# One set of 21 on-chip slots for keys, values, probability parts and tail loads in a quantised attention and mixture-of-experts layer

## The chip, the cores and the metric

The kernel runs on one core of a Trainium2 chip. The core has a matrix engine (PE, with its weight loads shown as PEld), a vector engine (DVE), a scalar engine (ACT), a general engine (POOL) and a sync engine (SP), each with its own instruction stream, and 16 DMA engines that all of them may start transfers on. The on-chip memory SBUF has 128 partitions; a tile's size is given here per partition. The metric is the time of one execution on the device in microseconds (us).

## What is computed

A layer over 2,048 tokens of width 256. `x` is normalised and projected to queries, keys and values of 16 heads of 128 with 4-bit weights (codes times scales of blocks of 32); softmax attention; an output projection; a normalisation and the residual. Then a router picks two of eight experts, each a gated feed-forward of inner width 176; their weighted sum is normalised and added.

```python
def attn(x, ...):
    q = _mxfp4_matmul(x, wq_codes, wq_scales) + bq      # k, v alike; 16 heads of 128
    scores = jnp.einsum('bqhd,bkhd->bhqk', q, k) / jnp.sqrt(jnp.float32(HEAD_DIM))
    attn = jax.nn.softmax(scores, axis=-1)
    out = jnp.einsum('bhqk,bkhd->bqhd', attn, v).reshape(B, S, NUM_HEADS * HEAD_DIM)
    return _mxfp4_matmul(out, wo_codes, wo_scales) + bo

def ffn(x, Wr, Wg, Wu, Wd):
    probs = jax.nn.softmax(jnp.einsum('bsh,he->bse', x, Wr), axis=-1)
    topk_w, topk_idx = jax.lax.top_k(probs, 2)
    combine = ...                                       # normalised, one-hot by expert
    h = jax.nn.silu(jnp.einsum('bsh,ehi->besi', x, Wg)) * jnp.einsum('bsh,ehi->besi', x, Wu)
    return jnp.einsum('bse,besh->bsh', combine, jnp.einsum('besi,eih->besh', h, Wd))

x = x + _layernorm(attn(_layernorm(x), ...))
x = x + _layernorm(ffn(_layernorm(x), ...))
```

## The kernel before

**Numbers in two parts.** Queries, keys, values and probabilities are each kept as a high and a low half-precision part whose sum carries more digits. So a score is three matmuls (high by high, high by low, low by high: L483, L484, L487), and so is a product with the values.

**The main loop** (L740) runs over 256 units and two more that drain it. Unit `g` is head `h = g // 16` and query tile `t = g % 16` of 128 rows. The order of instructions on every engine is the order in which the code issues them; nothing reorders them later. In each unit:

- PE computes the first half of the scores (1,024 keys) into a pair of accumulator banks `s`, of which there are three pairs; DVE takes its row maximum (L488).
- DVE forms the reciprocal of the sum of the unit before (`recip`, L506 to L509), and writes the second half of the low part `pl` of the unit before that (`low_half(1, ...)`, L528). Then SP issues the DMA transpose of that `pl` into `ptl` (L534).
- ACT writes the high part `ph` of the unit before (L513), and SP issues its transpose into `pth` (L516).
- PE computes the second half of the scores; DVE takes the maximum (L488) and combines the two (L492); ACT takes two exponentials into `p` (L499), which also frees the two score pairs.
- DVE writes the first half of the low part `pl` of the unit before (`low_half(0, ...)`, L528).
- PE works on parts of the product with the values (`pv_part`, L554): one for every half unit, eight to a block of four query tiles, 13 half units behind the scores. They read `pth`, `ptl` and `v`.
- `fill` puts projections between: in heads 0 to 14 the keys and values of a coming head, in all heads the next queries. PE computes them, ACT copies them to `t32` (L234, L265), POOL splits them into the two parts (L235, L236, L266, L267).

**Head 15** has no next keys and values to project. Instead `late` (L709) starts the loads of the tail: in units 0, 2, 4, 6, 8 a piece of the output weights (`wos` from ACT's queue in four DMAs, L632; `woc` from SP's, L637), in units 7, 9, 10, 11 the gate weights `Wg` (`gu_raw`, L673), in unit 9 the output bias `crow` (L724), and in units 9 and 11 to 14 finished head outputs read back from DRAM (`oi`, L693). ACT and POOL split the gate weights in units 10 to 13 (L664, L666). In the first draining unit SP issues three more `oi`.

**The tail** projects the outputs back (`op_mm`, L823), normalises, routes, and runs gate, up (L969) and down (L1009) matmuls for four blocks of 512 tokens. It loads `Wu` (`ust`), `Wd` (`draw`, L1112), `x` again (`x1`) and the other `oi`.

**Slots.** A tile comes from a pool under a tag; the tag has a fixed number of slots, each as large as the largest tile of the tag. When the program is built, each tile is given a slot of its tag that is then free. On the chip its first write waits, by a semaphore, until the slot's previous tile has been read for the last time; for a tile that a DMA reads, until that DMA has finished. Before the change these tags matter:

| tag | slots | KB of a slot | tiles |
|---|---|---|---|
| `kT` | 8 | 4 | keys of 512 positions, two parts (2 KB); in head 15 and the tail also `wos`, `woc`, `gu_raw`, `oi`, `x1_0` |
| `v` | 8 | 4 | values of 512 positions for two heads; later `wo`, `o_last`, `xT0`, `lgT0`, `x1_1`, `y`, one `oi` |
| `ph` | 3 | 4 | high part of the probabilities of a unit |
| `pl` | 2 | 4 | low part |
| `raw`, `at` | 2 and 2 | 4 | in the tail: `Wu` and `Wd` as loaded; the projected outputs |

`kT`, `v`, `ph` and `pl` are 21 slots of 4 KB together. The functions that the change touches and what calls them:

Of the kernel before, what the change touches and what calls it, by code (L numbers as in the profile page):

```python
# [20 lines left out]
S = 2048  # L21
# [9 lines left out]
ISQ = 1.0 / 128.0 ** 0.5  # L31
XS = 1024.0
PS = 16384.0
POOL_COLS = 512


@with_exitstack
def sandwich(
# [169 lines left out]
    def proj_psum(tag):  # L208
        if tag == "s":
            return s_pair()[:, 0]  # L210
        return psA.tile([128, 512], F32, name="pj", tag=tag)

    def proj_qk(which, h, b, tag="pj", wide=None):
        w = W[(h // 2, which)]
        bias = bqs[:, IX[which], h : h + 1]
        ps = proj_psum(tag)
        col = bass.ts(h % 2, 128)
        n = 0
        for kc in range(2):
            for hl in range(2):  # L220
                nc.tensor.matmul(
                    ps, w[:, kc, col], xnT[:, 4 * b : 4 * b + 4, hl * 2 + kc, :],
                    start=(n == 0), stop=(n == 3),
                )
                n += 1
        t = kqv.tile([128, 2, 512], HP, name=which + "T", bufs=8 if which == "k" else 2)
        if wide is None:
            nc.scalar.activation(t[:, 0, :], ps, AF.Identity, bias=bias)
            pending.append(lambda: nc.vector.scalar_tensor_tensor(
                t[:, 1, :], ps, bias, t[:, 0, :], ALU.add, ALU.subtract  # L230
            ))
        else:
            t32 = wide.tile([128, 512], F32, name="t32")
            nc.scalar.activation(t32, ps, AF.Identity, bias=bias)  # L234
            nc.gpsimd.tensor_copy(t[:, 0, :], t32)  # L235
            nc.gpsimd.tensor_tensor(t[:, 1, :], t32, t[:, 0, :], ALU.subtract)  # L236
        (Q if which == "q" else K)[(h, b)] = t

    def proj_v(p, t0, n, tag="pj", wide=None):
        w = W[(p, "v")]  # L240
        ps = proj_psum(tag)
        for j in range(n):
            i = 0
            for kc in range(2):
                for hl in range(2):
                    nc.tensor.matmul(
                        ps[:, bass.ts(j, 256)], xnT[:, t0 + j, hl * 2 + kc, :],
                        w[:, kc, :], start=(i == 0), stop=(i == 3),
                    )
                    i += 1  # L250
        if t0 % 4 == 0:
            V[(p, t0 // 4)] = kqv.tile([128, 2, 4, 256], HP, name="v", bufs=8)
        v = V[(p, t0 // 4)]
        sl = slice(t0 % 4, t0 % 4 + n)
        psv = ps[:, : n * 256].rearrange("p (t d) -> p t d", d=256)
        if wide is None:
            nc.scalar.copy(v[:, 0, sl, :], psv)
            pending.append(lambda: nc.vector.tensor_tensor(
                v[:, 1, sl, :], psv, v[:, 0, sl, :], ALU.subtract
            ))  # L260
        else:
            t32 = wide.tile([128, 512], F32, name="t32")[:, : n * 256].rearrange(
                "p (t d) -> p t d", d=256
            )
            nc.scalar.copy(t32, psv)  # L265
            nc.gpsimd.tensor_copy(v[:, 0, sl, :], t32)  # L266
            nc.gpsimd.tensor_tensor(v[:, 1, sl, :], t32, v[:, 0, sl, :], ALU.subtract)  # L267
# [241 lines left out]
        nc.vector.reciprocal(m[:, 6:7], m[:, 5:6])  # L509

    def high_part(h, t, m, p):
        ph = soft.tile([128, S], HP, name="ph", bufs=3)
        nc.scalar.activation(ph, p, AF.Copy, scale=m[:, 6:7])  # L513
        if t % 4 == 0:
            PT[(h, t // 4)] = pt.tile([128, 4, 16, 128], HP, name="pth")
        nc.sync.dma_start_transpose(  # L516
            out=PT[(h, t // 4)][:, t % 4], in_=ph
        )
        return ph
# [2 lines left out]

    def low_half(half, h, t, m, p, ph):
        if half == 0:
            LOW[(h, t)] = soft.tile([128, S], HP, name="pl")
        pl = LOW[(h, t)]
        cs = bass.ts(half, 1024)
        nc.vector.scalar_tensor_tensor(  # L528
# [17 lines left out]
    def pv_part(h, b, e):  # L546
# [10 lines left out]
            )  # L557
        if e == 7:
            if (h, b) == (NH - 1, 3):
                o = kqv.tile([128, 2, 2, 256], HP, name="o_last", tag="v", bufs=8)  # L560
                ps2 = halves(ps)
                nc.scalar.activation(o[:, :, 0, :], ps2, AF.Copy, scale=1.0 / PS)
                nc.vector.scalar_tensor_tensor(
# [76 lines left out]
    def dequant_wo(j):  # L640
        sc, cd = wo_raw.pop(j)
        if j % 4 == 0:
            wo.append(kqv.tile([128, 8, D], BF, name="wo", tag="v", bufs=8))
        hs = slice(2 * (j % 4), 2 * (j % 4) + 2)
        nc.gpsimd.tensor_tensor(wo[j // 4][:, hs], cd, sc, ALU.mult)

# [39 lines left out]

    OIN = {}

    def load_oi(b, half, j, tag="kT"):
        oi = kqv.tile(  # L690
            [128, 4, 2, 256], HP, name="oi", tag=tag, bufs={"kT": 8, "v": 8}[tag]
        )
        nc.sync.dma_start(  # L693
            out=oi.rearrange("p h l q -> p (h l q)"),
            in_=ot_d[b][:, half, 4 * j : 4 * j + 4].rearrange("p h l q -> p (h l q)"),
        )
        OIN[(b, half, j)] = oi
# [11 lines left out]
    def late(t):  # L709
        nonlocal gw, crow  # L710
        if t in WO_LOAD:
            load_wo(3 + WO_LOAD.index(t), kqv, ("kT", "kT"), 8)
        if t - 1 in WO_LOAD:
            dequant_wo(3 + WO_LOAD.index(t - 1))
        if t == 13:
# [10 lines left out]
            split_gu(gw, t - 10, gst.pop(t - 10), True)  # L726
        if t in WG_LOAD:
            i = WG_LOAD.index(t)
            gst[i] = load_gu(wg, i, kqv, "kT", 8)
        if t == 9:  # L730
            load_oi(0, 1, 0, "v")
        if 11 <= t < 15:
            load_oi(0, 0, t - 11)

# [5 lines left out]
    for g in range(NS + 2):  # L740
# [53 lines left out]
        if h == NH - 1:  # L794
            late(t)
        if g == NS:
            X1[0] = kqv.tile([128, 4, D], F32, name="x1_0", tag="kT", bufs=8)
            nc.sync.dma_start(out=X1[0], in_=XV[:, 0])
    UEND = 2 * (NS + 2)

# [10 lines left out]
    def op_mm(b, half, js, tag="pj"):  # L811
        if js[0] == 0:
            if half == 0:
                AT[b] = uwp.tile([128, 4, D], F32, name="at", bufs=2)
                MV[b] = small.tile([128, 4, 2], F32, name="mv")
            OPS[(b, half)] = aux_psum([128, 2, D], F32, "op", tag)
        ps = OPS[(b, half)]
# [54 lines left out]
    def tr(b, kc, tag="pj"):  # L872
        xn = AT[b]
        if kc == 0 and b == 0:
            XT[b] = [
                kqv.tile([128, 2, 512], F32R, name="xT0", tag="v", bufs=8)
                for _ in range(2)
            ]
        elif kc == 0:
# [11 lines left out]
    def router_a(b, tag="pj"):  # L891
# [7 lines left out]
                )  # L899
                n += 1  # L900
        if b == 0:
            LGT[b] = kqv.tile([8, 512], F32, name="lgT0", tag="v", bufs=8)
        else:
            LGT[b] = tl.tile([8, 512], F32, name="lgT", tag="sg", bufs=3)
        nc.scalar.copy(LGT[b], ps)
# [109 lines left out]
    YT = {}  # L1015

    def fin0(b):
        y = kqv.tile([128, 4, D], F32, name="y", tag="v", bufs=8)
        nc.scalar.copy(y, DPS.pop(b)[1])
        YT[b] = y  # L1020

# [17 lines left out]
            load_oi(b, i // 4, i % 4)  # L1039

    def fin_last(b):
        y = kqv.tile([128, 4, D], F32, name="y", tag="v", bufs=8)
        mv = small.tile([128, 4, 2], F32, name="mv3")
        r = []
        for half, dps in enumerate(DPS[b]):
# [24 lines left out]
    soft_ctx.close()  # L1070
    nc.scalar.activation(sgv, ssc[:, 0:1], AF.Sigmoid)
    uwp = ctx.enter_context(tc.tile_pool(name="uw", bufs=1, side="right", reuse_waits="tile"))
    ust = [load_gu(wu, i, uwp, "raw", 2) for i in range(2)]
    uw = uwp.tile([128, 2, 2, NCH, 128], F32R)
    for j in range(4):
        load_oi(1, 0, j)
# [13 lines left out]
    ln_c(0)  # L1090
    for i in range(2):
        split_gu(uw, i, ust[i], True)
        ust.append(load_gu(wu, i + 2, uwp, "raw", 2))
    for j in range(4):
        load_oi(1, 1, j)
    tr(0, 0, "s")
# [10 lines left out]
    dsrc = wd.rearrange("e i d -> (e i) d").rearrange("(p c) d -> p c d", c=NCH)  # L1107

    def load_d(c0):
        stg = uwp.tile([128, 4, D], F32, name="draw", tag="raw", bufs=2)  # L1110
        c1 = min(c0 + 4, NCH)
        nc.sync.dma_start(out=stg[:, : c1 - c0], in_=dsrc[:, c0:c1])  # L1112
        return stg, c0, c1
# [3 lines left out]

    def load_x1(b):
        if b == 1:
            X1[b] = kqv.tile([128, 4, D], F32, name="x1_1", tag="v", bufs=8)  # L1120
        else:
            X1[b] = tl.tile([128, 4, D], F32, name=f"x1_{b}")
        nc.sync.dma_start(out=X1[b], in_=XV[:, b])

    load_x1(1)
# [103 lines left out]
```

## Time and profile before

Three runs took 1849.41, 1852.74 and 1847.53 us. The profiled execution took 1847.86 us, of which its span, first to last instruction, is 1846.1 us.

| | us |
|---|---|
| median of three runs | 1849.41 |
| profiled execution | 1847.86 |
| span of the profile | 1846.1 |
| `pl` L528, 512 instructions | 722.9 busy, 1.412 each |
| exponentials L499, 512 | 612.2 busy, 1.200 each |
| `ph` L513, 256 | 513.0 busy, 2.004 each |
| maxima L488, 512 | 621.9 busy, 1.215 each |
| transposes L516 and L534, 256 each | 5.0 and 5.1 from issue to landing (median) |
| `oi` loads of 512 KB, 32 | 5.0 from issue to landing (median) |

Three lines of the page's list of the costliest groups show how it is read:

```profile
L528 DVE SCALAR_TENSOR_TENSOR pl<-p,m,ph 128x1024 f16<-128x1024 f32 x512 | 722.9, 1412 | 40.5 <-DMA ptl<-pl 39.7
L499 ACT ACTIVATE p<-s,m,ssc 128x1024 f32<-128x1024 f32 x512 | 612.2, 1200 | 182.7 <-DVE m L492 165.8
L513 ACT ACTIVATE ph<-p,m 128x2048 f16<-128x2048 f32 x256 | 513.0, 2004 | 69.6 <-issue 22.3
```

A line gives the source line, the engine, the operation, what it writes and reads (partitions by elements and type) and how often; after the first bar the busy time in us and the mean of one in ns; after the second the time that the engine stood idle just before these instructions and what ended most of it. So DVE stood 40.5 us before L528 instructions, and 39.7 of these ended when a transpose that reads `pl` landed. Idle time of an engine counts only where something that sets the end waits for that engine.

### The profile page before, as it was taken

What the parts mean: (1) busy time and instruction counts of PE and PEld (TensorE: products, weight loads), DVE (VectorE), ACT (ScalarE), POOL (GpSimd) and SP (SyncE); (2) the same over time, 40 slices, a digit from 0 to 9 for tenths busy, and PEclk for the clock granted to TensorE, in tenths of its full rate; (3) what the DMA queues carried; (4) which work ended last, traced back from release to release, by engine and by line L of the source; (5) the groups of instructions that cost most, each with busy time, mean ns of one, the idle gap of its engine ahead of it and who ended that gap; (6) DMA issues with size and microseconds to landing.
All of it is one profiled execution on the core that took longest, in us unless ns stands there. A gap on an engine that the chain in (4) does not pass through costs nothing. (4 is left out here: it accounts for less than half of the span.)

```text
span 1846.1 us, 25409 instructions
## 1 busy us (share of the span) xinstructions
PE 1780.4 (96%) x8890; PEld 934.0 (51%) x8890; DVE 1626.4 (88%) x2267; ACT 1369.7 (74%) x1730; POOL 948.7 (51%) x929
## 2 busy tenths in 40 slices
PE   6899999999999999999999999999999888899998
PEld 4344444444444444444444444444444334588887
DVE  7999999999999999999999999999999886468566
ACT  5788888888888888888888888888888776223232
POOL 3366566556655565556555556565446432333232
PEclk9999999999999999999999999999999999999999
DMA  2999999999999999999999999999999999851000
GB/s 84 175 203 201 196 202 202 196 198 201 202 192 198 196 198 193 209 193 202 194 197 200 196 197 206 191 201 200 191 192 199 207 215 230 246 192 35 1 12 23
DMA packets 1091504, 330.70 MB, mean 179 GB/s; under 512 B 1070048, under 2 KB 1078064, under 8 KB 1091376
## 3 DMA queue, kind: packets, MB, share of 16 engines
q1 hardware_dynamic: 1078688, 298.14, 88.1%
q0 software_dynamic: 10544, 29.40, 5.9%
q10 hardware_dynamic: 2144, 1.54, 0.3%
q8 instruction: 70, 1.15, 0.2%
q14 instruction: 58, 0.48, 0.1%
HBM read 41.68 MB, written 18.87 MB: 33 GB/s over the span
## 5 line engine op out<-in xcount | busy, mean ns | idle before, releaser
L528 DVE SCALAR_TENSOR_TENSOR pl<-p,m,ph 128x1024 f16<-128x1024 f32 x512 | 722.9, 1412 | 40.5 <-DMA ptl<-pl 39.7
L499 ACT ACTIVATE p<-s,m,ssc 128x1024 f32<-128x1024 f32 x512 | 612.2, 1200 | 182.7 <-DVE m L492 165.8
L488 DVE TENSOR_REDUCE m<-s 128x1 f32<-128x1024 f32 x512 | 621.9, 1215 | 16.9 <-PE s L487 16.1
L513 ACT ACTIVATE ph<-p,m 128x2048 f16<-128x2048 f32 x256 | 513.0, 2004 | 69.6 <-issue 22.3
L554 PE MATMUL pv<-pth,v 128*128 128x512 f16 x2048 | 506.0, 380 | 9.6 <-POOL v L267 4.7
L554 PEld LDWEIGHTS <-v 128*128 128x128 f16 x3072 | 301.1, 98 | 376.9 <-POOL v L267 7.7
L483 PE MATMUL s<-kT,qT 128*128 128x512 f16 x1024 | 388.9, 380 | 22.5 <-ACT p L499 21.2
L484 PE MATMUL s<-kT,qT 128*128 128x512 f16 x1024 | 388.9, 380 | 0.0
L487 PE MATMUL s<-kT,qT 128*128 128x512 f16 x1024 | 305.0, 379 | 0.0
L554 PE MATMUL pv<-ptl,v 128*128 128x512 f16 x1024 | 253.2, 380 | 0.0
L235 POOL CAST qT<-t 128x512 f16<-128x512 f32 x63 | 78.7, 1250 | 240.6 <-ACT t L234 240.6
L266 POOL CAST v<-t 128x256 f16<-128x256 f32 (+1 forms) x105 | 46.3, 441 | 263.8 <-ACT t L265 263.8
L484 PEld LDWEIGHTS <-qT 128*128 128x128 f16 x1024 | 100.2, 98 | 138.4 <-issue 34.6
L267 POOL TENSOR_TENSOR v<-t,v 128x256 f16<-128x256 f32 (+1 forms) x105 | 160.6, 1530 | 8.5
L487 PEld LDWEIGHTS <-qT 128*128 128x128 f16 x1024 | 100.3, 98 | 121.5 <-issue 1.1
L483 PEld LDWEIGHTS <-qT 128*128 128x128 f16 x1024 | 100.2, 98 | 110.0 <-issue 1.1
L984 POOL TENSOR_TENSOR hh<-sg,hh 128x512 fp32r<-128x512 f32 x42 | 55.1, 1313 | 141.1 <-ACT hh L983 106.1
L983 ACT CAST hh<-sg 128x512 fp32r<-128x512 f32 (+1 forms) x45 | 27.5, 611 | 107.1 <-DVE sg L995 107.0
L499 ACT ACTIVATION_READ_ACCUMULATOR p<-s,m,ssc 128x1 f32 x512 | 99.0, 193 | 0.0
L571 POOL TENSOR_TENSOR o<-t,o 128x512 f16<-128x512 f32 x63 | 96.2, 1527 | 5.2
L235 POOL CAST kT<-t 128x512 f16<-128x512 f32 x60 | 65.0, 1083 | 57.9 <-ACT t L234 57.9
L236 POOL TENSOR_TENSOR kT<-t,kT 128x512 f16<-128x512 f32 x60 | 86.3, 1438 | 5.1
(186 smaller groups left out, 1831.8 us busy)
## 6 DMA issues: line engine op xcount, KB each, us to landing
oi<-ot_d SPq DMA_DIRECT2D x32, 512.0 KB, 5.0
ot_d<-o POOLq DMA_DIRECT2D x63, 256.0 KB, 4.3
pth<-ph SPq DMA_TRANSPOSE x256, 5.0
ptl<-pl SPq DMA_TRANSPOSE x256, 5.1
xt<-in_L_attn_x SPq DMA_DIRECT2D x4, 512.0 KB, 4.0
x<-in_L_attn_x SPq DMA_DIRECT2D x4, 512.0 KB, 4.7
st_s<-in_L_attn_wv_scales POOLq DMA_DIRECT2D x28, 64.0 KB, 4.3
st_c<-in_L_attn_wv_codes POOLq DMA_DIRECT2D x14, 128.0 KB, 4.3
```

Source lines behind the costliest of these rows:

```text
L235: nc.gpsimd.tensor_copy(t[:, 0, :], t32)
L236: nc.gpsimd.tensor_tensor(t[:, 1, :], t32, t[:, 0, :], ALU.subtract)
L267: nc.gpsimd.tensor_tensor(v[:, 1, sl, :], t32, v[:, 0, sl, :], ALU.subtract)
L483: nc.tensor.matmul(s[:, j, :], q[:, 0, qc], k[:, 0, :], start=True, stop=False)
L484: nc.tensor.matmul(s[:, j, :], q[:, 0, qc], k[:, 1, :], start=False, stop=False)
L487: nc.tensor.matmul(s[:, j, :], q[:, 1, qc], k[:, 0, :], start=False, stop=True)
L488: nc.vector.tensor_reduce(m[:, half : half + 1], s, AX.XY, ALU.max)
L499: nc.scalar.activation(p[:, bass.ts(i, 1024)], s, AF.Exp, bias=m[:, 2:3], scale=ssc[:, 0:1], accum_out=m[:, 3 + i : 4 + i],)
L513: nc.scalar.activation(ph, p, AF.Copy, scale=m[:, 6:7])
L528: nc.vector.scalar_tensor_tensor(pl[:, cs], p[:, cs], m[:, 6:7], ph[:, cs], ALU.mult, ALU.subtract)
L554: nc.tensor.matmul(ps, V[(h // 2, c // 4)][:, i % 2, c % 4, dc], d[:, :, c, :], start=(n == 0), stop=(n == 47),)
L571: nc.gpsimd.tensor_tensor(o[:, :, 1, :], halves(t32), o[:, :, 0, :], ALU.subtract)
```

## The change

The tags `kT`, `v`, `ph`, `pl`, `raw` and `at` become one tag `x` with 21 slots of 4 KB in the pool `kqv`. Two blocks of 512 keys now share one tile of 4 KB: `kq_tile` makes it for an even block and returns its halves. The `x1` tiles of the third and fourth block of tokens, which had slots of their own, join as well. Nothing else in the program differs. The diff, with the hunks that only swap the tag of a tail tile left out (`o_last`, `wo`, `xT0`, `lgT0`, `y`, `x1_0`):

```diff
+NX = 21
...
+    KP = {}
+
+    def kq_tile(which, h, b):
+        if which == "q":
+            return kqv.tile([128, 2, 512], HP, name="qT", bufs=2)
+        if b % 2 == 0:
+            KP[h] = kqv.tile([128, 2, 2, 512], HP, name="kT", tag="x", bufs=NX)
+        return KP[h][:, b % 2]
+
     def proj_qk(which, h, b, tag="pj", wide=None):
...
-        t = kqv.tile([128, 2, 512], HP, name=which + "T", bufs=8 if which == "k" else 2)
+        t = kq_tile(which, h, b)
...
-            V[(p, t0 // 4)] = kqv.tile([128, 2, 4, 256], HP, name="v", bufs=8)
+            V[(p, t0 // 4)] = kqv.tile([128, 2, 4, 256], HP, name="v", tag="x", bufs=NX)
...
     def high_part(h, t, m, p):
-        ph = soft.tile([128, S], HP, name="ph", bufs=3)
+        ph = kqv.tile([128, S], HP, name="ph", tag="x", bufs=NX)
...
         if half == 0:
-            LOW[(h, t)] = soft.tile([128, S], HP, name="pl")
+            LOW[(h, t)] = kqv.tile([128, S], HP, name="pl", tag="x", bufs=NX)
...
-    def load_oi(b, half, j, tag="kT"):
+    def load_oi(b, half, j, tag="x"):
         oi = kqv.tile(
-            [128, 4, 2, 256], HP, name="oi", tag=tag, bufs={"kT": 8, "v": 8}[tag]
+            [128, 4, 2, 256], HP, name="oi", tag=tag, bufs=NX
         )
...
         if t in WO_LOAD:
-            load_wo(3 + WO_LOAD.index(t), kqv, ("kT", "kT"), 8)
+            load_wo(3 + WO_LOAD.index(t), kqv, ("x", "x"), NX)
...
-            gst[i] = load_gu(wg, i, kqv, "kT", 8)
+            gst[i] = load_gu(wg, i, kqv, "x", NX)
         if t == 9:
-            load_oi(0, 1, 0, "v")
+            load_oi(0, 1, 0, "x")
...
-                AT[b] = uwp.tile([128, 4, D], F32, name="at", bufs=2)
+                AT[b] = kqv.tile([128, 4, D], F32, name="at", tag="x", bufs=NX)
...
-    ust = [load_gu(wu, i, uwp, "raw", 2) for i in range(2)]
+    ust = [load_gu(wu, i, kqv, "x", NX) for i in range(2)]
...
-        ust.append(load_gu(wu, i + 2, uwp, "raw", 2))
+        ust.append(load_gu(wu, i + 2, kqv, "x", NX))
...
     def load_d(c0):
-        stg = uwp.tile([128, 4, D], F32, name="draw", tag="raw", bufs=2)
+        stg = kqv.tile([128, 4, D], F32, name="draw", tag="x", bufs=NX)
...
     def load_x1(b):
         if b == 1:
-            X1[b] = kqv.tile([128, 4, D], F32, name="x1_1", tag="v", bufs=8)
+            X1[b] = kqv.tile([128, 4, D], F32, name="x1_1", tag="x", bufs=NX)
         else:
-            X1[b] = tl.tile([128, 4, D], F32, name=f"x1_{b}")
+            X1[b] = kqv.tile([128, 4, D], F32, name=f"x1_{b}", tag="x", bufs=NX)
```

## The prediction, made before the changed kernel was run

> **What bounds the kernel now.** I read the page first, then the list of waits, first whole and then for two stretches, then a table by stage, the chain in order of time, and the timeline of single engines where the waits are longest. A unit below is one 128-row query tile of one head: two halves of scores (L483 to L487), two maxima (L488), two exponentials (L499), one `ph` (L513), two halves of `pl` (L528), two DMA transposes.
>
> ```profile
> PE 1780.4 (96%) x8890; PEld 934.0 (51%) x8890; DVE 1626.4 (88%) x2267; ACT 1369.7 (74%) x1730; POOL 948.7 (51%) x929
> ...
> DMA  2999999999999999999999999999999999851000
> ```
>
> PE is busy for 96% of the span and the DMA engines are full until the attention ends, so only stretches in which PE waits can shorten. The table by stage (us, then busy us of PE, PEld, DVE, ACT, POOL, granted clock, DMA share, GB/s) shows where that is:
>
> ```profile
> 222.00:410.00 188.00, 187.09 (x899) 87.61 (x897) 178.39 (x226) 160.10 (x201) 112.55 (x110) 1.00 1.09 198
> ...
> 1449.00:1519.00 70.00, 60.91 (x277) 26.86 (x276) 58.66 (x78) 51.64 (x62) 23.88 (x20) 1.00 1.12 214
> 1519.00:1569.00 50.00, 43.69 (x227) 22.33 (x226) 32.46 (x42) 34.55 (x39) 16.11 (x12) 0.93 1.12 224
> 1569.00:1600.00 31.00, 24.45 (x155) 15.12 (x153) 12.67 (x32) 4.27 (x5) 6.91 (x5) 0.94 1.05 300
> 1600.00:1846.00 246.00, 236.00 (x1486) 204.50 (x1484) 159.23 (x365) 69.67 (x119) 76.89 (x59) 0.99 0.17 58
> ```
>
> In the ordinary heads PE has 0.9 us idle in 188: PE is the bound. Head 15 (1449 to 1569) takes about 120 us where earlier heads take 93.5 to 96 (starts of L488, head by head), and PE, DVE and ACT all idle in it. The waits from 1425 to 1600 (total us, times, longest) say why:
>
> ```profile
> DVE pl L528 <- DMA ptl<-pl: 29.0, 14, 7.1
> ...
> PE s L483 <- ACT p L499: 17.5, 14, 5.2
> ...
> ACT ph L513 <- DMA pth<-ph: 4.0, 3, 2.3
> ...
> PE pv L554 <- DMA pth<-ph: 3.7, 1, 3.7
> ```
>
> `pl` has two buffers. Half 0 of unit t overwrites what the transpose of unit t-2 reads, so DVE stands until that transpose has landed. Behind it on DVE stand the maxima; behind those ACT's exponentials; behind those PE, which has no free score bank. The longest case, on DVE, SP and PE:
>
> ```profile
> 1524.16 0.27 DVE L492 TENSOR_SCALAR m<-m,ssc 128x1 f32<-128x1 f32 x1
> 1531.53 1.28 DVE L528 SCALAR_TENSOR_TENSOR pl<-p,m,ph 128x1024 f16<-128x1024 f32 x1 [7.10 <-DMA ptl<-pl]
> ```
> ```profile
> 1520.69 0.50 SPq L693 DMA_DIRECT2D oi<-ot_d  x1
> 1521.31 5.81 SPq L534 DMA_TRANSPOSE ptl<-pl  x1
> 1527.23 3.86 SPq L516 DMA_TRANSPOSE pth<-ph  x1
> ```
> ```profile
> 1538.34 0.58 PE L483 MATMUL s<-kT,qT 128*128 128x512 f16 x1 [5.18 <-ACT p L499]
> ```
>
> The transpose went in behind three loads (`crow`, `gu_raw`, `oi`), landed 10.1 us after its issue, and PE lost 5.2 us. The chain that ended last agrees (start, us):
>
> ```profile
> 1521.31 10.12 DMA ptl<-pl
> 1531.81 5.20 DMA ptl<-pl
> 1538.65 6.25 DMA ptl<-pl
> 1545.84 6.68 DMA ptl<-pl
> 1553.42 7.15 DMA ptl<-pl
> ```
>
> **The change, part by part.** No compute instruction or DMA is added, removed or reordered: the two built programs list the same instructions on each engine (SP 580, POOL 934, ACT 1247, DVE 2253, PE 16580). What moves is addresses, hence which earlier reader a first write waits for.
>
> *Removed: the two-buffer rule for `pl`.* I took each semaphore wait of the changed program, found the instruction that raises it, and gave both their times in the execution before. In the old program 42 of the 254 waits of L528 for an earlier `pl` transpose are met with under 0.5 us to spare, 194 with under 3 us. In the new one the tightest wait of L528 for a transpose has 6.3 us to spare (at 1567), the next 11.8 (at 1545).
>
> *Added: waits of the other kinds for slots.* By the same comparison all of them would be met at the old times: the tightest are `ph` 9.2 us (at 1523), first write of `v` 21.7, of a `kT` pair 23.5, `x1_1` 5.2, `oi` 3.4. A pair keeps its slot until both halves are read, and 4 KB slots that held 2 KB of keys are now filled; those margins contain that. So nothing new is late as long as nothing else moves: cost 0. The work that covers it is one to four units of 5.9 us between the last reader and the next writer. Should a landing come later than the margin, `pl` L528 is where it shows first, with the maxima, exponentials and scores behind it as before.
>
> *Added: more semaphore instructions,* 31 on ACT, 10 on DVE, 77 on POOL. They last 17 ns on ACT and POOL and 21 on DVE in this trace. POOL idles for half of the span. On the loop of DVE and ACT: 31 x 0.017 + 10 x 0.021 = 0.7 us.
>
> *Term A, up to 1425.* DVE waits there 10.7 us for `ptl`, in 13 places, but PE waits only 2.8 us behind them (L483 for L499, 4 times, longest 1.3). Bounds: 0 (PE catches up from queued `pv` work anyway) and -10.7. I take -2.8, since PE is the bound there.
>
> *Term B, 1425 to the last `pth` landing at 1580.6.* Three caps. (1) PE: its 17.5 us. (2) DVE and ACT: without slot waits a unit with `gw` casts takes 5.6 us (cast to cast on ACT, 1539.62 to 1545.23). In units 0 to 8 ACT also issues the `wos` loads (L632), which wait for the landing of `pth` on their semaphore; that stays. From one `ph` start to the next these five units took 8.04, 6.06, 6.33, 6.98 and 8.03 us, kept whole; the four between go from 24.6 to 4 x 5.6 = 22.4, so -2.2. Units 9 to 15 took 51.2 us and would take 7 x 5.6 = 39.2: -12.0. With the wait of 2.3 us at 1431: -16.5. (3) The DMA engines. From 1425 to 1581 they finished 89,682 packets of 256 B, which is 43.8 transposes of 2,048. In the ordinary heads 12 transposes in a row never took under 2.66 us each, 4 in a row seldom under 2.45 (the fastest hundredth), where the median is 2.94. The rest, by the usual time of a packet over 16 engines: 2,688 of 1 KB x 46 ns = 7.7 us, 2,048 of 704 B x 34 ns = 4.4, 1,617 of 4 KB x 162 ns = 16.4, together 28.5. So 43.8 x 2.66 + 28.5 = 145.0 of 156 us, -11.0; with 2.45, -20.2. The stretch needs 44 in a row, so 2.66 is nearer, and B = -11. Its weak end: the engines had packets in flight for all but 8 us from 1425 to 1585, so -8; its strong end is cap 2, -16.5.
>
> The Trainium skill (DMA: Bandwidth & Descriptors, Latency and other measured facts) gives 261 GB/s as the effective rate of a DMA transpose measured on one kernel. An estimate from that figure is 2.0 us for 512 KB; by it the third cap would be about -40 us and no cap at all, and the second would decide, for a time near 1831. The rows here are slower, and they decide.
>
> *The end.* After 1600 PE is busy for 236 of 246 us. The loads of `Wu`, `Wd`, `x` and `oi` that waited for their slots (L1112 alone held SP for 7.6 us) go out earlier, into a DMA share of 0.17, and nobody on PE was waiting for them: 0. Without that cover, one late `draw` would hold the splits and then `dps`.
>
> *The clock.* PE's 5.2 us of idle before 1538.3 lie beside a stretch of 6.8 us at half the granted clock (from 1537.2), the 3.7 us before 1580.7 beside one of 3.4 (from 1581.5). The first goes with its wait, in a place where PE isn't the bound. At the second PE will come earlier and may wait longer for the last `pth`: 0 to +1.7 us, and I take 0. The Trainium skill (TensorE: Matmul & The Clock Gate, Part 1) says that a PE idle for a window of some 3.4 us drops to half speed, which speaks for the +1.7.
>
> Sum, against the profiled execution's own 1847.86 us (span 1846.1): 1847.86 - 2.8 - 11.0 + 0.7 = 1834.8. The median of the runs shown is 1.55 us above that execution, so the forecast is 1836 us.
>
> **The rivals.** 0.3% is about what a measurement of this kernel tells from no change: 1843.9 to 1855.0.
>
> *It was hidden anyway: the DMA engines are the bound of head 15.* For it: a DMA share of 1.12 and only 8 us without packets. Then `pl` is no longer waited for, but the last `pth` lands hardly earlier, and PE's waits gather before L554 at the end: B = 0 to -3, A = -2.8, about 1845. Against it: the transposes came at 2.94 us each where 2.66 was sustained, and SP itself stood for `pl` (12.8 us from 1425 to 1600). Chance 0.15.
>
> *The engines gain all of it.* Transposes run at 2.45 us and cap 2 decides: B = -16.5, A up to -5, so 1847.86 - 21.5 + 0.7 + 1.55 = 1828.6. For it: while DVE waits, SP holds `pth` behind the unfinished `ptl`, so some of the DMA time is made by the wait. Against it: the `wos` waits on ACT, and eight loads of 512 KB in units 9 to 16. Chance 0.13.
>
> *Slower: loads and transposes mix.* The `ptl` transposes issued beside loads at 1521 and at 1569 took 10.1 and 10.3 us to land, against a median of 6.7 in that stretch. With nothing to hold DVE, more transposes are pending when the six loads of `gu_raw` and `oi` of units 10 to 14 go out. If each lost the same 3.5 us, 21 us would be lost where at most 12 are gained: +9, with A and the semaphores +7, so 1856. It decides once the median landing of `ptl` from 1519 on exceeds about 9 us. Against it: SP's order is fixed, and these loads already stand directly before a transpose that landed in 6 to 7 us. Chance 0.07.
>
> **How the numbers follow.** The forecast has 0.65, with its own range from B = -16.5 to -8 and A = -5 to 0: 1829 to 1842. The range of 8 in 10 takes in the larger gain and all but the worst of the hidden case: 1828 to 1846. Faster by over 0.3%: 0.65 + 0.13 = 0.78; within: 0.15; slower: 0.07.
>
> **What would show it.** L528's waits for `ptl` under 3 us in all, from 39.7. L483's waits for L499 under 6, from 21.2. Head 15 nearer to 100 than to 120 us. In place of them a longer wait of L554 for `pth` at the end of the attention, its landing some 11 to 14 us earlier than 1580.6. Stage after 1600 unchanged within 2 us. The forecast is wrong if the last `pth` lands within 3 us of its old time, if L528 or L513 waits for slots again, or if transposes of head 15 land later than before.

## The result, and the profile after

The changed kernel takes 1838.64 us (median of 7 runs, 1836.61 to 1840.73), the kernel before 1845.91 us (7 runs, 1840.31 to 1852.74): ratio 0.9958, 95% interval 0.9939 to 0.9976, some 7 us faster. The profiled execution took 1840.48 us with a span of 1838.7 us, 7.4 us less than the 1846.1 us of before. In the changed kernel's listing the lines of the loop and the tail stand 9 further down: `pl` is L537 (was L528), the transposes L525 and L543 (L516, L534), the scores L492 (L483), the exponentials L508 (L499), the product with the values L563 (L554), `wos` L641 (L632).

The two lines of the page's list of costliest groups that answer to those of before, `pl` on DVE and the first scores on PE:

```profile
L537 DVE SCALAR_TENSOR_TENSOR pl<-p,m,ph 128x1024 f16<-128x1024 f32 x512 | 723.9, 1414 | 12.5 <-ACT ph L522 12.1
...
L492 PE MATMUL s<-kT,qT 128*128 128x512 f16 x1024 | 389.0, 380 | 11.8 <-ACT p L508 11.2
```

DVE's 39.7 us of waiting for transposes that read `pl` are gone. What stands before `pl` now is a wait for `ph`, 12.1 us, and 11.9 of these lie between 1425 and 1600 us, where there was no such wait before: in head 15 `ph` itself is now late. PE's wait for the exponentials has gone from 21.2 to 11.2 us. Yet 28 us less idle on DVE made the kernel only 7 us shorter. The table by stage shows where these 7 us came from. I cut both spans at the first maximum of head 1, of head 14 and of head 15, and at the landing of the last `pth`. Columns: stretch, its length, then busy us of PE, PEld, DVE, ACT, POOL with the number of instructions, granted clock, DMA share (it adds up the packets' times, so it can pass 1), GB/s. The kernel before:

```profile
128.50:1354.20 1225.70, 1217.67 (x5825) 569.14 (x5824) 1163.53 (x1457) 1037.83 (x1294) 716.55 (x711) 1.00 1.09 198
1354.20:1449.30 95.10, 92.22 (x434) 42.06 (x432) 88.19 (x113) 79.34 (x98) 53.42 (x53) 1.00 1.09 200
1449.30:1580.60 131.30, 111.53 (x562) 54.83 (x560) 94.65 (x130) 85.89 (x100) 41.27 (x32) 0.97 1.13 221
1580.60:1846.10 265.50, 253.22 (x1576) 213.86 (x1576) 168.07 (x385) 73.94 (x123) 82.50 (x63) 0.98 0.23 78
```

The changed kernel, cut at the same events:

```profile
129.20:1348.30 1219.10, 1215.12 (x5825) 568.68 (x5824) 1162.68 (x1457) 1038.27 (x1294) 722.70 (x711) 1.00 1.10 199
1348.30:1441.30 93.00, 92.23 (x434) 42.13 (x433) 88.10 (x114) 79.10 (x97) 54.08 (x53) 1.00 1.09 200
1441.30:1571.80 130.50, 111.56 (x562) 54.69 (x560) 96.20 (x130) 85.53 (x100) 41.31 (x32) 0.96 1.12 225
1571.80:1838.70 266.90, 254.42 (x1576) 214.19 (x1576) 169.81 (x385) 73.69 (x123) 81.78 (x63) 0.98 0.21 77
```

Heads 1 to 13 give 1225.7 - 1219.1 = 6.6 us and head 14 gives 2.1. From the start of head 15 to the last landing, where nearly the whole gain was forecast, it is 0.8. The stretch behind that loses 1.4, and the start, which the change doesn't touch, was 0.7 longer in this execution. The sum is -7.4.

So in head 15 the wait was removed and the time was not. PE's largest waits there in the changed kernel (start, us, then in brackets the idle time just before and what ended it):

```profile
1506.72 0.58 PE L492 MATMUL s<-kT,qT 128*128 128x512 f16 x1 [2.97 <-ACT p L508]
1539.71 4.62 PE L563 MATMUL pv<-pth,v 128*128 128x512 f16 x12 [5.32 <-ACT p L508]
...
1571.81 8.23 PE L563 MATMUL pv<-pth,v 128*128 128x512 f16 x24 [3.08 <-DMA pth<-ph]
```

The 5.18 us that PE lost before scores at 1538 in the old kernel have become 5.32 us before the product with the values at 1539.71. The bracket names ACT, but a transpose into `pth` landed at 1539.62 and that exponential was long done: it is a wait for a transpose again, this time from the reader's side. And ACT shows waits of 2.1 to 3.8 us before `ph` in each unit with `wos` loads, the longest of them here:

```profile
1501.16 2.22 ACTq L641 DMA_DIRECT2D wos<-in_L_attn_wo_scales  x2
1503.48 2.00 ACT L522 ACTIVATE ph<-p,m 128x2048 f16<-128x2048 f32 x1 [3.75 <-DMA gu_raw<-in_L_ffn_Wg]
```

`ph` reads no `gu_raw`. In front of it in ACT's order stand the last two `wos` issues, which went out at 1501.16 and 1503.04; the second of them waited on a semaphore that it shares with a load of `gu_raw`, and that one rose at 1503.01. The five units with `wos` grew from 35.4 to 40.5 us together (from one `ph` start to the next), the four between them shrank from 24.6 to 19.6: 60.0 us before, 60.1 after. Units 9 to 15 did shrink, from 51.2 to 46.8 us, but from the start of the last `ph` to the landing of its transpose it then took 21.4 us in place of 18.3. That leaves two readings of head 15, the DMA engines or ACT's issues, told apart below.

### The profile page after: what moved, and what is told of

It reads as the page before. It is cut to its first block, busy times and chain, and to the rows that moved or that the text cites. A ratio compares the mean times of both kernels' runs of the same rounds, so it can differ in the third digit from the quotient of the medians.

```text
span 1838.7 us, 25522 instructions
## 1 busy us (share of the span) xinstructions
PE 1780.5 (97%) x8890; PEld 934.2 (51%) x8890; DVE 1628.9 (89%) x2267; ACT 1369.4 (74%) x1730; POOL 954.2 (52%) x929
## 5 line engine op out<-in xcount | busy, mean ns | idle before, releaser
L508 ACT ACTIVATE p<-s,m,ssc 128x1024 f32<-128x1024 f32 x512 | 611.7, 1199 | 183.3 <-DVE m L501 177.2
L537 DVE SCALAR_TENSOR_TENSOR pl<-p,m,ph 128x1024 f16<-128x1024 f32 x512 | 723.9, 1414 | 12.5 <-ACT ph L522 12.1
L563 PE MATMUL pv<-pth,v 128*128 128x512 f16 x2048 | 509.1, 382 | 13.6 <-ACT p L508 5.3
L563 PEld LDWEIGHTS <-v 128*128 128x128 f16 x3072 | 301.1, 98 | 382.8 <-issue 12.4
L492 PE MATMUL s<-kT,qT 128*128 128x512 f16 x1024 | 389.0, 380 | 11.8 <-ACT p L508 11.2
L563 PE MATMUL pv<-ptl,v 128*128 128x512 f16 x1024 | 252.0, 379 | 0.0
L492 PEld LDWEIGHTS <-qT 128*128 128x128 f16 x1024 | 100.1, 98 | 110.4 <-issue 1.8
L508 ACT ACTIVATION_READ_ACCUMULATOR p<-s,m,ssc 128x1 f32 x512 | 99.1, 194 | 0.0
```

The costliest lines, as they stand in the source:

```text
L492: nc.tensor.matmul(s[:, j, :], q[:, 0, qc], k[:, 0, :], start=True, stop=False)
L508: nc.scalar.activation(p[:, bass.ts(i, 1024)], s, AF.Exp, bias=m[:, 2:3], scale=ssc[:, 0:1], accum_out=m[:, 3 + i : 4 + i],)
L537: nc.vector.scalar_tensor_tensor(pl[:, cs], p[:, cs], m[:, 6:7], ph[:, cs], ALU.mult, ALU.subtract)
L563: nc.tensor.matmul(ps, V[(h // 2, c // 4)][:, i % 2, c % 4, dc], d[:, :, c, :], start=(n == 0), stop=(n == 47),)
```

## Experiments

The theories. T1: the gain in the ordinary heads comes from `pl` having more than two slots, and from nothing else in the common set. R1: the common set for the other tiles and the tail's loads brings it. For head 15, H1: the DMA engines are the bound (the rival "it was hidden anyway" of the prediction). H2: ACT's `wos` issues are.

Each ratio is to runs of the kernel before in the same session, whose medians were 1845.91 us for the changed kernel, 1848.1 for e1 to e4, 1847.46 for e5 to e7 and 1847.74 for e8 and e9. Across sessions the ratios compare better than the medians.

| run | median us | ratio to the kernel before | 95% interval | span of its profile |
|---|---|---|---|---|
| changed kernel | 1838.64 | 0.9958 | 0.9939 to 0.9976 | 1838.7 |
| e1, `pl` in two slots | 1847.87 | 0.9995 | 0.9982 to 1.0007 | 1850.4 |
| e2, `pl` in three, no common set | 1838.95 | 0.9948 | 0.9929 to 0.9966 | 1835.7 |
| e3, no transposes of `pl` in head 15 | 1816.02 | 0.9828 | 0.9806 to 0.9849 | 1813.1 |
| e4, `wos` issued by POOL | 1841.67 | 0.9966 | 0.9955 to 0.9977 | 1836.6 |
| e5, `crow` early | 1838.41 | 0.9944 | 0.9930 to 0.9957 | 1836.6 |
| e6, output weights early | 1830.69 | 0.9906 | 0.9891 to 0.9921 | 1835.0 |
| e7, these, `crow` and gate weights early | 1831.19 | 0.9919 | 0.9904 to 0.9935 | 1824.5 |
| e8, the same, spread | 1836.06 | 0.9943 | 0.9922 to 0.9963 | 1830.7 |
| e9, as e8, `oi` earlier | 1833.43 | 0.9931 | 0.9910 to 0.9953 | 1833.0 |

### e1: `pl` back in two slots

```diff
-NX = 21
+NX = 19
...
-            LOW[(h, t)] = kqv.tile([128, S], HP, name="pl", tag="x", bufs=NX)
+            LOW[(h, t)] = soft.tile([128, S], HP, name="pl")
```

> The changed kernel, but `pl` keeps two slots of its own and the common set has 19; all else stays in the common set. T1 (the whole gain comes from `pl` having more than two slots): the gain is gone, 1844 to 1848 us, ratio to the kernel before 0.999 to 1.001, and DVE waits for `ptl` before the writes of `pl` for some 40 us again. R1 (the common set for the other tiles and the tail's loads brings the gain): 1837 to 1841 us, ratio about 0.996, though DVE waits.

The ratio is 0.9995 with 1.000 inside its interval: the gain is gone. Two lines of its page, and its heads 1 to 13 from the table by stage:

```profile
L537 DVE SCALAR_TENSOR_TENSOR pl<-p,m,ph 128x1024 f16<-128x1024 f32 x512 | 725.7, 1417 | 40.2 <-DMA ptl<-pl 38.1
...
L492 PE MATMUL s<-kT,qT 128*128 128x512 f16 x1024 | 388.5, 379 | 24.0 <-ACT p L508 22.8
```
```profile
129.70:1359.20 1229.50, 1218.87 (x5825) 569.06 (x5824) 1163.86 (x1457) 1038.44 (x1294) 712.11 (x711) 1.00 1.09 198
```

With 19 common slots for everything else, DVE's 38.1 us of waiting for `ptl` and PE's 22.8 us are back as before. T1 holds, R1 falls. In the stretch of heads 1 to 13 the two kernels with two slots take 1225.7 and 1229.5 us, the changed kernel, e3, e4 and e5 1219.1 to 1219.5.

### e2: the kernel before, with a third slot for `pl`

```diff
+        if b % 2 == 0:
+            KP[h] = kqv.tile([128, 2, 2, 512], HP, name="kT", bufs=7)
+        return KP[h][:, b % 2]
...
-            LOW[(h, t)] = soft.tile([128, S], HP, name="pl")
+            LOW[(h, t)] = soft.tile([128, S], HP, name="pl", bufs=3)
```

> The kernel before with the least edit that gives `pl` a third slot: keys in pairs, 7 slots for them in place of 8, `pl` with 3 slots; no common set. T1: a third slot is all that is needed, 1837 to 1841 us, ratio about 0.996, DVE's waits for `ptl` under 3 us. R1: 1844 to 1848 us, ratio about 1.000. In between (DVE's waits under 3 us before head 15 but 5 us or more in head 15, ratio 0.997 to 0.999): three slots are enough in the ordinary heads and the common set adds the rest in head 15.

```profile
L537 DVE SCALAR_TENSOR_TENSOR pl<-p,m,ph 128x1024 f16<-128x1024 f32 x512 | 723.7, 1414 | 12.2 <-ACT ph L522 8.1
...
L492 PE MATMUL s<-kT,qT 128*128 128x512 f16 x1024 | 389.0, 380 | 10.6 <-ACT p L508 10.0
```
```profile
127.40:1348.40 1221.00, 1215.66 (x5825) 568.91 (x5824) 1162.42 (x1457) 1037.94 (x1294) 720.91 (x711) 1.00 1.10 199
1348.40:1442.10 93.70, 92.50 (x434) 42.12 (x432) 88.84 (x113) 79.20 (x97) 53.30 (x53) 1.00 1.11 203
1442.10:1568.90 126.80, 112.04 (x560) 55.31 (x559) 96.53 (x131) 85.65 (x100) 41.82 (x32) 0.96 1.10 230
```

One slot more does all that the common set does: 0.9948, an interval that overlaps that of the changed kernel, nearly the same two lines of the page, heads 1 to 13 in 1221.0 us. From the start of head 15 to the last landing (the third row) this execution took 126.8 us, against 130.5 in the changed kernel and 131.3 and 131.8 with two slots (before, e1). So what head 15 gained is known only as 1 to 5 us, from one execution of each kernel. The pairs of keys are what pays for it: they turn eight half-used slots into seven, and the eighth goes to `pl`. The common set itself adds nothing that these runs can tell.

### e3: no transposes of `pl` in head 15

```diff
+            if h == NH - 1:
+                PTL[(h, t // 4)] = PTL[(NH - 2, 3)]
+                LOW.pop((h, t))
+                return
```

> The changed kernel without the 16 transposes of `pl` in head 15: the products of head 15 with the values read the transposed low part of the last block of head 14 for all four blocks, so this part of the computation is left out. PE has the same matmuls. H1 (the DMA engines are the bound of head 15): 16 transposes of about 2.7 us are 43 us of DMA work less, so the last `pth` lands 10 us or more before 1571.8 us and the whole takes 1827 us or less. H2 (ACT's issues of `wos`, which wait for the landing of `pth`, set units 0 to 8): these units still take 57 us or more from the `ph` of the unit before to the `ph` of unit 8 (60.1 in the changed kernel); what is gained lies in units 9 to 15 and is under 7 us; 1832 us or more.

```profile
1440.00:1542.50 102.50, 99.66 (x490) 47.28 (x488) 90.90 (x119) 85.86 (x100) 42.93 (x30) 1.00 0.97 208
```

This is the start of head 15 to the last landing of `pth`: 102.5 us in place of 130.5, with PE busy for 99.7 of them. Units 0 to 8 took 51.9 us where H2 had 57 or more, though the `wos` issues stayed on ACT. H1 holds against H2: with 16 transposes fewer PE, DVE and ACT run freely, and the kernel ends 22.6 us earlier by the medians. From the packets in flight one can also read what a transpose costs the DMA engines. I count a moment with n packets in flight as n sixteenths of work, and at most as one. By this count, from 24 us before head 15 to the last landing, the engines had work for 145.5 us in the changed kernel with 44.3 transposes, and for 108.7 us here with 29.4, so (145.5 - 108.7) / 14.9 = 2.47 us each.

e3 also takes 16 issues off SP, so alone it doesn't tell the DMA engines from SP's issuing. Against SP: its shortest row for a transpose is 1.32 us, half of the 2.6 us at which the transposes came, and the 16 engines were idle for only 9.0 of 154.5 us. No run moved the transposes to another engine's queue.

### e4: `wos` issued by POOL

```diff
-            nc.scalar.dma_start(
+            nc.gpsimd.dma_start(
```

> The changed kernel with the four `wos` loads of a piece issued by POOL and no more by ACT; their bytes and their place in the code stay. H2 (ACT stands at these issues): units 0 to 8 of head 15 take 50 to 55 us in place of 60.1, ACT's waits of 2.1 to 3.8 us before `ph` are gone, the last `pth` lands 3 us or more earlier and the time falls to 1836 us or less. H1 (the DMA engines are the bound): units 0 to 8 may be shorter but the transposes land later after them; last `pth` within 2 us of 1571.8, time within 2 us of the changed kernel.

The table by stage, cut at the `ph` of unit 8 and the last landing. The changed kernel:

```profile
1443.40:1503.50 60.10, 53.58 (x245) 23.81 (x244) 52.92 (x66) 42.61 (x51) 21.26 (x17) 1.00 1.16 217
1503.50:1571.80 68.30, 56.02 (x310) 30.11 (x307) 41.64 (x60) 41.34 (x46) 20.05 (x15) 0.92 1.09 232
```

e4, and PE's largest entry in its list of waits from 1440 to 1575 (total us, times, longest):

```profile
1441.50:1496.10 54.60, 50.36 (x224) 22.16 (x223) 48.34 (x64) 42.91 (x50) 26.79 (x30) 0.97 1.13 209
1496.10:1571.70 75.60, 61.39 (x331) 32.50 (x328) 44.99 (x63) 41.55 (x47) 23.95 (x22) 0.93 1.10 232
```
```profile
PE pv L563 <- DMA pth<-ph: 15.7, 4, 5.3
```

Units 0 to 8 are 5.5 us shorter and ACT waits no more before `ph`; then the second part is 7.3 us longer, and the last `pth` lands at 1571.7, where the changed kernel has 1571.8. (This execution came to head 15 2 us earlier; from there it took 132.4 us against 130.5.) The median is 3.0 us above the changed kernel's, more than the 2 us that H1 allowed, but the ratios, 0.9966 and 0.9958, have intervals that overlap; H2's 1836 us or less is excluded. In place of PE's waits for exponentials there are four waits for `pth`, one for each block of four query tiles. So when ACT was no longer held, the wait moved from the writer of the buffer to the reader of the result. The Trainium skill (Trainium Kernel Development and Optimization, Key Constraints) says that DMAs issued from SP, ACT and POOL all run on the same 16 DMA engines and that issuing from several engines only saves the issue time of the sequencer; these rows agree.

### e5 to e7: loads taken out of head 15

e5 loads `crow` in head 0:

```diff
+            nc.gpsimd.dma_start(out=crow, in_=bo.partition_broadcast(128))
...
-            nc.sync.dma_start(out=crow, in_=bo.partition_broadcast(128))
```

> The changed kernel with the output bias `crow` loaded in head 0 by POOL in place of unit 9 of head 15. H1 (the DMA engines are the bound from 1417 to the last `pth` landing): its 128 packets of about 400 ns are 3.2 us of the 16 engines' time, so the last `pth` lands 2 to 4 us earlier after the start of head 15 (130.5 us in the changed kernel) and the time falls to 1835 to 1837 us. H2 (a single late transpose in front of which `crow` stood): unit 10 is shorter, but later units take it back, under 1 us.

From the start of head 15 to the last landing it took 130.8 us, not less, and unit 10 took 6.2 us against 6.3. H1's price was a misreading: in the changed kernel the 128 packets of `crow` took 53 ns in the median and 0.8 us of the 16 engines' time together, in the kernel before 206 ns and 1.8 us. So small an effect can't be seen here; the ratio, 0.9944, overlaps the changed kernel's.

e6 takes all output weights out of head 15; each piece goes through `load_wo_part`, which head 14 uses for three of them:

```diff
+        w = 4 * (h - NH + 3) + t // 4
+        if 0 < w <= 8 and t % 4 == 0:
+            dequant_wo(w - 1)
+        if 0 <= w < 8 and t % 4 < 3:
+            load_wo_part(w, t % 4)
...
-        if t in WO_LOAD:
-            load_wo(3 + WO_LOAD.index(t), kqv, ("x", "x"), NX)
-        if t - 1 in WO_LOAD:
-            dequant_wo(3 + WO_LOAD.index(t - 1))
```

> The changed kernel with all eight pieces of the output weights loaded and converted in heads 13 and 14 by POOL, none in head 15 (five there before, 2,560 packets of 1 KB, by the usual time of a packet 7.4 us of the 16 engines' time). H1: from the start of head 15 to the last `pth` landing 122 to 125 us in place of 130.5, time 1830 to 1834 us; heads 13 and 14 stay at 93.5 to 94.7 us, as they have 8 us of DMA time to spare each. H3 (the work only moves: the transposes of heads 13 and 14 are late in turn): heads 13 and 14 grow by 3 us or more together and the time stays above 1836 us.

e7 adds `crow` as in e5, and the gate weights:

```diff
+        if h == NH - 2 and t in (9, 11, 13, 15):
+            i = (t - 9) // 2
+            gst[i] = load_gu(wg, i, kqv, "x", NX, nc.gpsimd)
```

> As e6, and `crow` in head 0 and the four loads of the gate weights in head 14 (units 9, 11, 13, 15) by POOL. In all 15 us of DMA work are taken out of the stretch from 1417 to the last `pth` landing. H1: start of head 15 to last `pth` landing 114 to 119 us, time 1823 to 1829 us, the maxima, exponentials and `ph` wait for nothing that a DMA holds in units 0 to 9. H3 (the work only moves): head 14 grows by 3 us or more, or the common set runs out of slots and DVE waits for `ptl` again, time above 1831 us.

Heads 13 and 14 together, then head 15 to the last landing, first in the changed kernel, then e6, then e7:

```profile
1253.70:1441.30 187.60, 186.73 (x886) 86.43 (x885) 179.18 (x225) 158.55 (x195) 101.95 (x99) 1.00 1.09 196
1441.30:1571.80 130.50, 111.56 (x562) 54.69 (x560) 96.20 (x130) 85.53 (x100) 41.31 (x32) 0.96 1.12 225
```
```profile
1251.50:1443.50 192.00, 187.62 (x883) 86.38 (x882) 176.04 (x225) 159.28 (x196) 126.48 (x129) 0.99 1.15 205
1443.50:1568.10 124.60, 112.53 (x565) 55.44 (x563) 94.04 (x130) 85.77 (x100) 34.94 (x27) 0.96 1.12 217
```
```profile
1251.90:1445.80 193.90, 188.34 (x882) 86.52 (x881) 176.16 (x224) 159.06 (x195) 127.44 (x133) 0.98 1.14 212
1445.80:1557.50 111.70, 108.16 (x566) 54.78 (x564) 94.50 (x130) 85.82 (x100) 36.02 (x27) 1.00 1.14 224
```

Head 15 shortens as H1 says, by 5.9 us in e6 and by 18.8 in e7, more than H1 asked there. With `crow` at 0.8 us, e7's loads are some 12.6 us and not 15. By the count of e3, the engines had 3.7 and 13.1 us less work from 24 us before head 15 to the last landing, and their idle time there fell from 9.0 to 6.8 and to 3.2 us. e6 also takes the `wos` issues off ACT; e4 shows that this alone doesn't shorten head 15. But H3 is right in part: heads 13 and 14 grow by 4.4 and 6.3 us, and e7's 1831.19 us lies outside the 1823 to 1829 of H1. By the medians both beat the changed kernel by 7 to 8 us, with intervals below its own; between the two these runs can't choose. e7's profiled execution was the fastest of its five runs (1826.25, against up to 1835.82), e6's the slowest of its own, so their spans don't compare with the medians.

### e8 and e9: the same loads spread

Most of what heads 13 and 14 lose is a single stall with the half-clock stretch beside it, here in e7 on PE:

```profile
1435.14 2.72 PE L565 MATMUL pv<-pth,v 128*128 128x512 f16 x6 [3.61 <-DMA pth<-ph]
```

The transpose that it waited for went out beside four `wos` loads and one of `gu_raw`. e8 moves `gu_raw` and two of the four `wos` away from it (the other two still went out while it was in flight):

```diff
+    WG_LOAD = (7, 11, 15, 19)
...
-        w = 4 * (h - NH + 3) + t // 4
+        w, part = divmod(g - (NH - 3) * NT - 1, 4)
...
-        if h == NH - 2 and t in (9, 11, 13, 15):
+        if g - (NH - 2) * NT in WG_LOAD:
```

> As e7, but the pieces of the output weights go out one unit later in each block of four, and the gate weights in units 7, 11, 15 of head 14 and 3 of head 15, so that they don't go out beside the transpose of `ph` that the first product with the values of a block waits for (in e7 it landed at 1434.9 after 6.5 us and PE stood 3.6 us, with 6.8 us at half clock after it). If that collision is what head 14 lost in e7: heads 13 and 14 take 93.3 to 95 us each, start of head 15 to last `pth` landing 112 to 118 us, time 1820 to 1828 us. If the DMA engines have no room in heads 13 and 14 at all: another block boundary stands in its place, head 13 and 14 together 5 us or more longer than 188, time 1829 us or more.

```profile
1436.96 2.31 PE L565 MATMUL pv<-pth,v 128*128 128x512 f16 x6 [3.53 <-DMA pth<-ph]
```
```profile
1254.10:1446.70 192.60, 187.24 (x882) 86.31 (x881) 178.56 (x224) 158.75 (x195) 120.14 (x132) 0.99 1.13 210
1446.70:1563.80 117.10, 108.26 (x566) 54.44 (x564) 95.66 (x130) 85.79 (x100) 36.98 (x28) 1.00 1.13 219
```

My theory of a collision of neighbours got no support: with three neighbours fewer the stall stands in the same unit with the same 3.5 us, heads 13 and 14 take 192.6 us, and the median is no better than e7's. As two `wos` stayed beside the transpose, it isn't excluded either. The second reading, that heads 13 and 14 have no room for all this, fits the 1836.06 us; but it asked for a stall at another block boundary, which didn't come, and for 193 us or more. Its own run (loads spread over more heads) was not tried, so it is not shown.

e9 moves three `oi` loads to units 3, 5 and 8 of head 15:

```diff
-        if t == 9:
-            load_oi(0, 1, 0, "x")
+        if t in (3, 5, 8):
+            load_oi(0, 1, (3, 5, 8).index(t))
...
-            load_oi(0, 1, 1)
-            load_oi(0, 1, 2)
```

> As e8, and three of the four `oi` of the second half of block 0 go out in units 3, 5 and 8 of head 15 in place of one in unit 9 and two directly before the last transposes (2.6 us of DMA work moved off the end of the stretch). If the DMA engines are full up to the last transposes: from the start of the last `ph` to its landing 2 to 3 us less than in e8 and the time 1 to 3 us below e8. If units 0 to 9 have no room: these units grow by as much, and the time stays within 1 us of e8.

From the start of the last `ph` to the last landing it took 20.3 us, against 22.8 in e8, as the first reading asks; but units 9 to 15 grew from 40.6 to 43.8 us, so from the start of head 15 to the last landing it took 117.0 us against 117.1. Units 0 to 9, where the second reading looked for the growth, did not grow. The median is 2.6 us below e8's with intervals that overlap: inconclusive.

## Why the prediction came out as it did

The forecast of 1836 us was 2.6 us below the median, in the right direction and inside its range. That nearness is in part luck. The gain that was forecast is 13.4 us, from the 1849.41 us then on record; over seven runs the kernel before has 1845.91 us, and the gain is 7.3. The range of 1828 to 1846 holds 1845.91 too, so it could not tell a gain from none. Between the two profiled executions the forecast was -13.1 us and -7.4 came: term A was 5.9 us too small and term B 10.2 us too large, errors in opposite directions, and for head 15 the rival was nearer.

*The removed rule and the new waits: right.* L528's wait for `ptl` went from 39.7 us to nothing, and no slot wait of another kind took its place; e1 and e2 show that this is the whole effect of the change, as far as their intervals tell. The 0.7 us for semaphores is too small to be seen.

*Term A, forecast -2.8 us: too small.* The heads up to head 15 gave 6.6 + 2.1 = 8.7 us (the forecast drew the line between A and B at 1425, 24 us before head 15; I draw it at the start of the head, which both traces show). The step that failed is the choice between the bounds 0 and -10.7: I took PE's listed waits for L499 as the whole cost. The lists of waits from the start of head 1 to that of head 15, before (total us, times, longest):

```profile
DVE pl L528 <- DMA ptl<-pl: 13.0, 14, 2.6
...
PE s L483 <- ACT p L499: 4.8, 5, 2.1
PE pv L554 <- POOL v L267: 4.7, 7, 0.8
```

and on PE in the changed kernel:

```profile
PE pv L563 <- POOL v L276: 4.1, 7, 0.6
PE s L492 <- ACT p L508: 0.2, 1, 0.2
```

So the time fell by two thirds of what DVE had waited, 8.7 of 13.0 us, and the listed waits for exponentials by 4.6. By the table by stage PE's idle time there fell from 10.9 to 4.8 us, and its matmul records, the same number, were 2.5 us shorter in sum. What made the records longer before was not traced, so for these 2.5 us the cause stays open.

*Term B, forecast -11 us: too large.* From the start of head 15 to the last landing it was -0.8, and in e2, with the same rule removed, 126.8 - 131.3 = -4.5; both fall short of the weak end of -8. Of the three caps the third, the DMA engines, was the right one, and its rate too: with the 28.5 us of other packets taken off, the changed kernel's transposes came at (154.5 - 28.5 - 9.0) / 44.3 = 2.64 us, where 2.66 was taken. What failed is that the idle time of the DMA engines would vanish, which even the weak end of -8 assumed. By the count of e3 they were idle for 7.7 us in the stretch before and for 9.0 after. PE's stops at the end of a block, for `pth`, delay the next `ph`, and then there is for a moment nothing to transpose; this loop is my reading of the rows and not shown. For it: in e7, where PE doesn't stop for `pth` in head 15 before the end, the engines were idle for 3.2 us.

*The `wos` units kept whole: wrong, and without weight.* They grew by 5.1 us, while the four between them fell by 5.0 where 2.2 was forecast. e4 took ACT's waits away and the last landing stayed.

*The Trainium skill's rate for transposes* (DMA: Bandwidth & Descriptors, Latency and other measured facts), 261 GB/s, gave an estimate of 2.0 us for 512 KB, by which the DMA engines would be no bound. The 2.47 us of e3 are 212 GB/s, so measurement decides against it here.

*The end and the clock.* The stretch behind the last landing was to stay within 2 us; it grew by 1.4. The table by stage at the last landing, the changed kernel:

```profile
1570.80:1577.70 6.90, 5.89 (x14) 2.09 (x15) 4.46 (x14) 0.00 (x0) 1.23 (x2) 0.51 1.08 266
```

and the kernel before:

```profile
1581.50:1585.00 3.50, 3.50 (x10) 1.25 (x9) 2.71 (x6) 0.00 (x0) 0.00 (x0) 0.51 1.09 243
```

The stretch at a clock of 0.51 lasts 6.9 us in place of 3.5. PE was busy for 5.89 us of it and for 3.50 before; at half speed that loses 2.9 and 1.75 us, so some 1.2 us more. It wasn't a longer wait of PE that did it: that was 3.08 us, against 3.67 before. Nor was it the change: in e2 and e4, where DVE's waits for `ptl` are gone too, the stretch at the end is again 3.4 us. The Trainium skill (TensorE: Matmul & The Clock Gate, Part 1) says that the window of some 3.4 us runs freely and isn't started by the kernel. The traces agree: the changed kernel's half-clock stretches start at 1505.99, 1536.71 and 1570.84, which is 9 and 10 times 3.413 us apart. So whether the clock term is 0 or near its bound of +1.7 depends on how PE's wait falls on this grid, which the forecast could not know; the last section has the figures.

*What would show it.* Right: the waits for `ptl`, no new slot waits, the last stretch. Wrong: L483's wait (11.2 us, not under 6), head 15 nearer to 100 than to 120 us, the last landing 11 to 14 us earlier (8.9, nearly all of it made before head 15), and a longer wait at its end (3.08 us, not above 3.67). PE's longest wait for `pth` came at the end of an earlier block, at 1539.71.

*The rivals.* "Hidden anyway" priced head 15 rightly for the changed kernel (0 to -3; e2's -4.5 lies outside) and named the bound that e3 and e4 support; its 1845 us failed with term A, which it shared. "The engines gain all of it" is excluded by the same runs. "Loads and transposes mix" was to decide above a median landing of 9 us late in head 15; it was 6.3.

## What to carry to other kernels

A DMA that reads a buffer holds the buffer until it has landed; where that takes about as long as a step of the loop (here 5.1 us in the median, and up to 10.3 in head 15, against 5.9 us), two slots make the writer wait at times; here one more slot was all that was needed, so try the smallest number of slots before building a common set. Before pricing such a wait in a stretch where the DMA engines are nearly always busy, ask whether they could do the work sooner: if not, the wait moves to the reader of the result, and here only less DMA work in that stretch helped. In a stretch where one engine is busy for 99%, a delay upstream can cost more than the waits listed on that engine: here 4.8 us were listed on PE, DVE had waited 13.0, and 8.7 came off the time.

## What the runs showed of the hardware that was not expected

The half-clock stretches of PE (granted clock 0.5) follow a grid of time. In the ten traces that have such stretches between 1300 and 1600 us (all but e3) there are 28; within a trace their starts lie whole multiples of 3.413 us apart, and 19 last 3.41 us and 9 last 6.83. I cut the traces from 300 to 1790 us into windows on this grid and added up PE's gaps of over 0.15 us in each. At full speed the clock fell after every window in which PE stood idle for 2.03 us or more, and after none with 2.01 us or less. So a window need not be idle from end to end: 2 of 3.4 us were enough. A half-clock stretch ended after its first window where PE was idle in it for 0.73 us or less, and went on for a second one from 0.81 us. At the end of the attention that was 0.97 us in the changed kernel and none before.

A packet's time in flight is not set by the load alone: the same 128 packets of `crow` took 206 ns in the median in the kernel before and 53 ns in the changed kernel. A price for a load that is read from one trace needn't hold in the next.
